# Score products of a causal attention, cut into two halves of 64 weight columns

## The chip, the cores and the metric

The kernel runs on one core of a Trainium2 chip. The metric is the device time of one execution in microseconds (us), taken as the median of several runs.

## The reference

The program is one block of a "macaron" transformer in f32: half a feed-forward step, attention, half a feed-forward step. The input x is 4 sequences of 1024 rows with 256 features.

```python
x = x + 0.5 * _L0_ffn_ref(_layernorm(x, axis=-1), ...)
x = x + _L0_attn_ref(_layernorm(x, axis=-1), ...)
x = x + 0.5 * _L0_ffn_ref(_layernorm(x, axis=-1), ...)

# in _L0_attn_ref: 16 heads of 16 features, rotary embedding on q and k
att = jnp.einsum('bhqd,bhkd->bhqk', q, k) / math.sqrt(hd)
mask = jnp.triu(jnp.full((T, T), -jnp.inf, dtype=att.dtype), k=1)
att = jax.nn.softmax(att + mask, axis=-1)
out = jnp.einsum('bhqk,bhkd->bhqd', att, v)
```

The feed-forward step is silu(x gate) * (x up), 704 wide, times a down matrix, with a scale for each output. What matters here is the product `q k` for each head, which contracts over only 16 features.

## The kernel before

**Tiling.** The 4096 rows are 8 blocks of 512 (`BLK`), two to a sequence. Heads lie in groups of four (`g`, 0 to 3): each head has 32 partitions (`HP`), of which 16 hold its features (`HD`). The tiles `qT` and `kT` hold queries and keys of a block in that form, features on partitions and rows on the free axis. In `qT`, a seventeenth row holds the negated maximum of each query's scores, and `kT` holds ones there.

**Scores are computed twice.** `max_half` computes scores with the query on the output partition, so that VectorE can take the maximum along the free axis: the weights are 128 columns of `qT`, the stream is up to 512 columns of `kT`. The maxima are turned by a small product (L939), copied, and sent into row 17 of `qT` by DMA. `exp_half` then computes the scores with the key on the output partition: the weights are 128 columns of `kT` with their row of ones, the stream is `qT`, and the maximum is subtracted by the product itself. ScalarE takes the exponential out of PSUM into `pT` (L981). `weigh` (L1019) multiplies `pT` with the values `va`, `attended` divides by the totals, and `project` applies Wo.

A unit of work covers four streams of 512 columns, one for each head of a group: a half has two heads (`pair` 0 or 1, `e` 0 or 1), and a burst places two halves of different pairs, so that the four heads' products stand on four different 32-row strips of TensorE. A half has one entry of 512 columns, or two entries (384 and 128, or 256 and 256) that share a PSUM bank. Each head's scores go to a bank of their own, `sc[e]`.

**The other products** go through `product_of`, which cuts the weights of 128 columns into four products of 32 columns (L470). These are the feed-forward products, the projections to q, k and v, and Wo. The products of `weigh` also have 32 weight columns, one head each. So TensorE works in two shapes for nearly the whole kernel: 32 rows by 128 columns for scores, 128 rows by 32 columns for the rest.

**Order.** The order of all instructions is fixed when the kernel is built. A planner (`Planner`) keeps an assumed clock for each engine, takes operations with an assumed duration `us`, and always places the one that can start first. For TensorE it adds assumed costs for a change between the shapes (`CHANGE`), and `burst` decides which two halves form the next visit to the scores: it waits for four free PSUM banks, and tends to place two bursts in a visit (`VISIT`). `plan.place` calls the operation's `emit`, which issues the instructions. The assumed duration of a half is `mm_us` of its columns. All of this is the same before and after the change.

The names that the change touches are `emit` in `max_half` (matmul at L859) and `emit` in `exp_half` (matmul at L972).

Of the kernel before, what the change touches and what calls it, by code (L numbers as in the profile page):

```python
# [19 lines left out]
P = 128  # L20
# [207 lines left out]
def mm_us(cols):  # L228
    return 4 * cols / 2400


def dve_us(n):
    return n / 960 + 0.07


def act_us(n, ptr=0):
    return n / 1200 + 0.09 + 0.09 * ptr
# [3 lines left out]
def tile_macaron(  # L241
# [16 lines left out]
    nc = tc.nc  # L258
# [9 lines left out]
    BLK = 512  # L268
    NB = BLK // P
# [7 lines left out]
        x=(6, [P, NB, D]),  # L277
        qT=(2, [P, NG, BLK]),
# [188 lines left out]
    def product_of(out, w, x, **kw):  # L467

        for m in range(w.shape[1] // HP):
            nc.tensor.matmul(out[ts(m, HP)], w[:, ts(m, HP)], x, **kw)  # L470

    def idle(d, n):

        for _ in range(n):
            nc.tensor.matmul(d.tile[:, :P], ident, ident, start=True, stop=True)
# [36 lines left out]
    def turned(pair, j, xnT, prio, later, view, idles=0):  # L512

        ds = [Buf("d") for _ in range(NC)]

        def emit():
            idle(ds[0], idles)
            for c, d in enumerate(ds):
                for n, (xn, _) in enumerate(pair):
                    nc.tensor.transpose(d.tile[:, ts(n, P)], xn.tile[:, ts(c, P)], ident)  # L520

        def copy(c):
            (nc.vector.tensor_copy if c else nc.scalar.copy)(
                view(xnT.tile[:, c])[:, j - 1 : j + 1],
                ds[c].tile[:, : 2 * P].rearrange("p (j a t) -> p j a t", j=2, t=HP),
            )

        t = Op("pe", 4 * 0.107, emit, [p[1] for p in pair], [*ds, xnT], [p[0] for p in pair], prio=prio, mode="full")
        k = [Op("act", act_us(D), partial(copy, 0), [t], uses=[ds[0], xnT], prio=later)]
        return t, [*k, Op("dve", dve_us(D), partial(copy, 1), [t], uses=[ds[1], xnT], prio=later)]  # L530
# [156 lines left out]
    qT = [Buf("qT") for _ in range(NBLK)]  # L687
# [156 lines left out]
    def row_at(g, part, h, j):  # L844

        return g % 2 * HP + part * GH * NB + h * NB + j

    def max_half(blk, unit, pair, nm, reduces):

        parts = 1 + blk % BPS  # L850
        sc = [Buf("score") for _ in range(2)]
        tiles = [kT[blk - parts + 1 + u[2]] for u in unit]

        def emit():

            for (g, j, _, c0, w, _), kt in reversed(list(zip(unit, tiles))):
                for e in range(2):
                    r = slice((2 * pair + e) * HP, (2 * pair + e) * HP + HD)
                    nc.tensor.matmul(  # L859
                        sc[e].tile[:, c0 : c0 + w],  # L860
                        qT[blk].tile[r, g, ts(j, P)],
                        kt.tile[r, g, :w],
                        start=True,
                        stop=True,
                    )

        gs = {u[0] // 2 for u in unit}
        need = [T_done[1, b, n] for b in range(blk - blk % BPS, blk + 1) for n in gs]
        first = Op(
            "pe", mm_us(sum(u[4] for u in unit)), emit, need, [*sc, nm], [qT[blk], *tiles], mode="row", tail=0.25  # L870
        )
        masked = [(c0 + w - P, c0 + w) for _, _, _, c0, w, m in unit if m]

        def head(e):
            prev = first
            if masked:

                def mask():
                    a, z = masked[0][0], masked[-1][1]
                    if masked[0][1] == masked[-1][0] or len(masked) == 1:  # L880
                        d = sc[e].tile[:, a:z].rearrange("p (m k) -> p m k", k=P)
                    else:
                        d = sc[e].tile.rearrange("p (m k) -> p m k", k=2 * P)[:, :, P:]
                    nc.vector.tensor_tensor(d, d, causal.unsqueeze(1).to_broadcast([P, len(masked), P]), ALU.add)  # L884

                prev = Op("dve", dve_us(P * len(masked)), mask, [first], uses=[sc[e]], prio=0, tail=0.1)
                loose_att.append(prev)

            if unit[0][0] != unit[-1][0]:
                j, part = unit[0][1:3]  # L890

                def reduce():
                    o = row_at(0, part, 2 * pair + e, j)
                    nc.vector.tensor_reduce(  # L894
                        nm.tile[:, o : o + HP + 1 : HP],
                        sc[e].tile.rearrange("p (g k) -> p g k", g=2),
                        AX.X,
                        ALU.max,
                        negate=True,
                    )  # L900

                o = Op("dve", dve_us(BLK), reduce, [prev, *filled["nm"]], uses=[sc[e], nm], prio=0, tail=0.25)
                loose_att.append(o)
                for g in (unit[0][0], unit[-1][0]):
                    reduces[g].append(o)
            else:
                for g, j, part, c0, w, _ in unit:

                    def reduce(g=g, j=j, part=part, c0=c0, w=w):
                        o = row_at(g, part, 2 * pair + e, j)  # L910
                        nc.vector.tensor_reduce(  # L911
                            nm.tile[:, o : o + 1], sc[e].tile[:, c0 : c0 + w], AX.X, ALU.max, negate=True
                        )

                    o = Op("dve", dve_us(w), reduce, [prev, *filled["nm"]], uses=[sc[e], nm], prio=0, tail=0.25)
                    loose_att.append(o)
                    reduces[g].append(o)

        for e in range(2):
            head(e)  # L920
        first.pair, first.kind = pair, "max"
        return first
# [38 lines left out]
    def exp_half(blk, unit, pair, pT, masks):  # L961
        base = blk - blk % BPS
        diag0 = blk % BPS * NB
        sc = [Buf("score") for _ in range(2)]
        tiles = [kT[base + k // NB] for _, k, _, _ in unit]
        w = sum(x[3] for x in unit)

        def emit():
            for (g, k, c0, w), kt in reversed(list(zip(unit, tiles))):
                for e in range(2):  # L970
                    r = slice((2 * pair + e) * HP, (2 * pair + e) * HP + HD + 1)
                    nc.tensor.matmul(  # L972
                        sc[e].tile[:, c0 : c0 + w],
                        kt.tile[r, g, ts(k % NB, P)],
                        qT[blk].tile[r, g, BLK - w :],
                        start=True,
                        stop=True,
                    )

        def weights(e):  # L980
            nc.scalar.activation(pT.tile[:, e, :w], sc[e].tile[:, :w], AF.Exp)  # L981

        need = [row_done[blk, g, pair] for g in sorted({u[0] for u in unit})]
        first = Op("pe", mm_us(w), emit, need, [*sc, pT], [qT[blk], *tiles], mode="row", tail=0.25)
        last = [Op("act", act_us(w), partial(weights, e), [first], uses=[sc[e], pT], prio=0, tail=0.25) for e in range(2)]
        loose_att.extend(last)
        done = list(last)
        for _, k, c0, _ in unit:
            if k >= diag0:

                def mask(c0=c0):
                    d = pT.tile[:, :, c0 : c0 + P]
                    nc.gpsimd.affine_select(  # L993
                        out=d,
                        in_=d,
                        compare_op=ALU.is_ge,
                        fill=0.0,
                        base=0,
                        pattern=[[0, 2], [1, P]],
                        channel_multiplier=-1,  # L1000
                    )

                last.append(Op("pool", 0.45, mask, done, uses=[pT], prio=0))
                loose_att.append(last[-1])
        masks.extend(last)
        first.pair, first.kind = pair, "exp"
        return first
# [297 lines left out]
```

## Time and profile before

| what | value |
|---|---|
| median of 3 runs | 1046.38 us (1046.28 to 1048.42) |
| profiled execution, its time | 1046.28 us |
| its span, first to last instruction | 1044.4 us |
| TensorE products: busy, instructions | 1036.3 us, 12162 |
| TensorE weight loads: busy, instructions | 442.7 us, 12162 |
| VectorE busy | 808.5 us |
| ScalarE busy | 429.7 us |
| GpSimd busy | 295.1 us |
| granted TensorE clock | 1.0 |

In the profile, PE stands for TensorE's products, PEld for its weight loads (issued by the same queue, able to overlap products), DVE for VectorE, ACT for ScalarE, POOL for GpSimd and SP for the queue that issues most DMAs. A group of instructions is written as line, engine, operation, output tile <- input tiles, then the shape: "17*128 17x512 f32" is a product with 17 rows and 128 columns of weights and 512 streamed columns. After the count come the busy time in us, the mean length of one in ns, and the time for which the engine was idle before them with what ended it. The length of a product counts from its own start to the modelled end of its last column, so products that follow each other closely overlap in the record.

### The profile page before, as it was taken

What the parts mean: (1) busy time and instruction counts of PE and PEld (TensorE: products, weight loads), DVE (VectorE), ACT (ScalarE), POOL (GpSimd) and SP (SyncE); (2) the same over time, 40 slices, a digit from 0 to 9 for tenths busy, and PEclk for the clock granted to TensorE, in tenths of its full rate; (3) what the DMA queues carried; (4) which work ended last, traced back from release to release, by engine and by line L of the source; (5) the groups of instructions that cost most, each with busy time, mean ns of one, the idle gap of its engine ahead of it and who ended that gap; (6) DMA issues with size and microseconds to landing.
All of it is one profiled execution on the core that took longest, in us unless ns stands there. A gap on an engine that the chain in (4) does not pass through costs nothing.

```text
span 1044.4 us, 28697 instructions
## 1 busy us (share of the span) xinstructions
PE 1036.3 (99%) x12162; PEld 442.7 (42%) x12162; DVE 808.5 (77%) x1876; ACT 429.7 (41%) x821; POOL 295.1 (28%) x501
## 2 busy tenths in 40 slices
PE   9999999999999999999999999999999999999998
PEld 5434443343444444443434443342434443434443
DVE  6679889788898887888897798778896797884432
ACT  3314341444453452435454434544354444455411
POOL 5222542231121633312115424221226211112200
PEclk9999999999999999999999999999999999999999
DMA  7211202102020021111010103101012010010000
GB/s 290 62 42 38 66 3 62 42 2 62 22 42 23 12 61 34 37 48 22 32 52 8 37 2 72 32 13 52 3 38 50 22 39 22 12 52 3 21 22 22
DMA packets 37969, 41.10 MB, mean 39 GB/s; under 512 B 3985, under 2 KB 27729, under 8 KB 37713
## 3 DMA queue, kind: packets, MB, share of 16 engines
q1 hardware_dynamic: 37184, 38.81, 14.1%
q8 instruction: 95, 1.56, 0.6%
q10 hardware_dynamic: 656, 0.47, 0.2%
q14 instruction: 34, 0.27, 0.1%
HBM read 19.60 MB, written 15.20 MB: 33 GB/s over the span
## 4 chain that ended last, share of the span: by engine, by line
PE 92%; DVE 6%; DMA 1%; issue 0%; ACT 0%; SPq 0%; DVEq 0%
PE bank L470 54%; PE bank L859 17%; PE bank L1019 12%; PE bank L972 10%; DVE nm L911 1%; DVE bank L884 1%; DVE xs L491 1%; DVE nm L894 1%; PE bank L939 0%; DVE hT L626 0%; DVE ta L623 0%; DMA xd<-xs 0%; PE bank L520 0%; DVE ta L603 0%; DVE hL L606 0%
## 5 line engine op out<-in xcount | busy, mean ns | idle before, releaser
L981 ACT ACTIVATE pT<-bank 128x512 f32<-128x512 f32 x576 | 298.5, 603 | 307.5 <-PE bank L972 306.7
L911 DVE TENSOR_REDUCE nm<-bank 128x1 f32<-128x512 f32 (+2 forms) x640 | 330.3, 573 | 20.0 <-PE bank L972 17.8
L470 PE MATMUL bank<-xnT,wgu_sb 128*32 128x512 f32 (+1 forms) x2832 | 321.5, 592 | 0.3
L859 PE MATMUL bank<-kT,qT 16*128 16x512 f32 (+3 forms) x1536 | 286.8, 511 | 2.2 <-DVE x L1104 0.9
L972 PE MATMUL bank<-qT,kT 17*128 17x512 f32 (+3 forms) x1536 | 286.7, 514 | 0.0
L470 PEld LDWEIGHTS bank<-xnT,wgu_sb 128*32 128x32 f32 x2832 | 92.0, 109 | 194.6 <-issue 122.1
L993 POOL TENSOR_SCALAR_AFFINE_SELECT pT<-pT 128x256 f32<-128x256 f32 x256 | 99.1, 407 | 263.9 <-ACT pT L981 263.0
L859 PEld LDWEIGHTS bank<-kT,qT 16*128 16x128 f32 x1536 | 111.3, 184 | 141.7 <-issue 35.3
L470 PE MATMUL bank<-wd_sb,hT 128*32 128x256 f32 x2560 | 152.4, 379 | 0.0
L1019 PE MATMUL bank<-pT,va 128*32 128x512 f32 (+3 forms) x1536 | 137.5, 487 | 0.4 <-DVE nm L911 0.2
L884 DVE TENSOR_TENSOR bank<-bank,causal 128x256 f32<-128x256 f32 (+1 forms) x320 | 103.9, 370 | 20.3 <-PE bank L972 15.1
L972 PEld LDWEIGHTS bank<-qT,kT 17*128 17x128 f32 x1536 | 109.4, 184 | 9.4 <-issue 2.6
L470 PEld LDWEIGHTS bank<-wd_sb,hT 128*32 128x32 f32 x2560 | 85.4, 110 | 55.1 <-issue 2.6
L620 ACT ACTIVATE ta<-bank,gus_sb 128x512 f32<-128x512 f32 x80 | 55.0, 687 | 113.2 <-PE bank L470 100.8
L623 DVE SCALAR_TENSOR_TENSOR ta<-ta,bank 128x512 f32<-128x512 f32 x80 | 54.6, 683 | 44.4 <-ACT ta L620 43.6
L1019 PEld LDWEIGHTS bank<-pT,va 128*32 128x32 f32 x1536 | 51.7, 109 | 83.5 <-issue 59.9
L1058 POOL TENSOR_TENSOR oq<-oq 128x512 f32<-128x512 f32 x32 | 40.7, 1273 | 154.8 <-DVE oq L1055 151.9
L1055 DVE STREAM_TRANSPOSE oq<-bank 128x512 f32<-128x512 f32 x64 | 45.5, 711 | 35.1 <-PE bank L1019 34.5
L626 DVE SCALAR_TENSOR_TENSOR hT<-bank,gus_sb,ta 128x512 f32<-128x512 f32 x80 | 59.5, 744 | 16.7 <-PE bank L470 15.5
L652 DVE TENSOR_TENSOR x<-bank,x 128x256 f32<-128x256 f32 x64 | 26.8, 418 | 49.7 <-PE bank L470 49.3
L731 POOL TENSOR_TENSOR qs<-qs,rope_sb 128x512 f32<-128x512 f32 x32 | 40.8, 1277 | 79.7 <-DVE qs L728 60.0
L470 PE MATMUL bank<-xnT,wqkv_sb 128*32 128x512 f32 x512 | 60.6, 595 | 0.1
(61 smaller groups left out, 649.0 us busy)
## 6 DMA issues: line engine op xcount, KB each, us to landing
xd<-xs SPq DMA_DIRECT2D x84, 128.0 KB
xnT<-xd SPq DMA_DIRECT2D x21, 512.0 KB
kT<-qT SPq DMA_DIRECT2D x64, 64.0 KB
x<-in_x SPq DMA_DIRECT2D x7, 512.0 KB
out<-x SPq DMA_DIRECT2D x14, 256.0 KB
qT<-nmT SPq DMA_DIRECT2D x128, 2.0 KB
wgu_sb<-in_wgu SPq DMA_DIRECT2D x2, 512.0 KB
rope_sb<-in_rope SPq DMA_DIRECT2D x1, 1024.0 KB
```

The lines of the kernel that those rows point to most:

```text
L470: nc.tensor.matmul(out[ts(m, HP)], w[:, ts(m, HP)], x, **kw)
L620: nc.scalar.activation(a.tile, d.tile, AF.Tanh, scale=gus_sb[:, 0, c : c + 1])
L623: nc.vector.scalar_tensor_tensor(a.tile, a.tile, 1.0, d.tile, ALU.add, ALU.mult)
L626: nc.vector.scalar_tensor_tensor(hT[c].tile, e.tile, gus_sb[:, 1, c : c + 1], a.tile, ALU.mult, ALU.mult)
L859: nc.tensor.matmul(sc[e].tile[:, c0 : c0 + w], qT[blk].tile[r, g, ts(j, P)], kt.tile[r, g, :w], start=True, stop=True,)
L884: nc.vector.tensor_tensor(d, d, causal.unsqueeze(1).to_broadcast([P, len(masked), P]), ALU.add)
L911: nc.vector.tensor_reduce(nm.tile[:, o : o + 1], sc[e].tile[:, c0 : c0 + w], AX.X, ALU.max, negate=True)
L972: nc.tensor.matmul(sc[e].tile[:, c0 : c0 + w], kt.tile[r, g, ts(k % NB, P)], qT[blk].tile[r, g, BLK - w :], start=True, stop=True,)
L981: nc.scalar.activation(pT.tile[:, e, :w], sc[e].tile[:, :w], AF.Exp)
L993: nc.gpsimd.affine_select(out=d, in_=d, compare_op=ALU.is_ge, fill=0.0, base=0, pattern=[[0, 2], [1, P]], channel_multiplier=-1,)
L1019: nc.tensor.matmul(av.tile[ts(r, HP), BLK - w :], va[base + k // NB].tile[:, k % NB, h * VS : h * VS + HP], pTs[u, r // 2].tile[:, r % 2, ...
L1055: nc.vector.transpose(o.tile, av.tile)
```

## The change

A helper `scores` is added beside `product_of`. It issues a score product as two products with 64 weight columns each, the first into output partitions 0 to 63, the second into 64 to 127. Rows, streamed columns and PSUM bank stay the same. A burst of four heads then stands on eight tiles of 32 rows and 64 columns. Both score products call it; the planner's assumed durations are not changed.

```diff
+    def scores(out, w, x):
+
+        for m in range(2):
+            nc.tensor.matmul(out[ts(m, P // 2)], w[:, ts(m, P // 2)], x, start=True, stop=True)
+
...
                 for e in range(2):
                     r = slice((2 * pair + e) * HP, (2 * pair + e) * HP + HD)
-                    nc.tensor.matmul(
-                        sc[e].tile[:, c0 : c0 + w],
-                        qT[blk].tile[r, g, ts(j, P)],
-                        kt.tile[r, g, :w],
-                        start=True,
-                        stop=True,
-                    )
+                    scores(sc[e].tile[:, c0 : c0 + w], qT[blk].tile[r, g, ts(j, P)], kt.tile[r, g, :w])
...
                     r = slice((2 * pair + e) * HP, (2 * pair + e) * HP + HD + 1)
-                    nc.tensor.matmul(
-                        sc[e].tile[:, c0 : c0 + w],
-                        kt.tile[r, g, ts(k % NB, P)],
-                        qT[blk].tile[r, g, BLK - w :],
-                        start=True,
-                        stop=True,
-                    )
+                    scores(sc[e].tile[:, c0 : c0 + w], kt.tile[r, g, ts(k % NB, P)], qT[blk].tile[r, g, BLK - w :])
```

## The prediction

> **What bounds the kernel now.** I read the engine totals first, then the chain, then the groups of TensorE with shapes kept apart, then a timeline of one stretch of score products. The page says that TensorE is the bound from end to end:
>
> ```profile
> PE 1036.3 (99%) x12162; PEld 442.7 (42%) x12162; DVE 808.5 (77%) x1876; ACT 429.7 (41%) x821; POOL 295.1 (28%) x501
> ...
> PE 92%; DVE 6%; DMA 1%; issue 0%; ACT 0%; SPq 0%; DVEq 0%
> PE bank L470 54%; PE bank L859 17%; PE bank L1019 12%; PE bank L972 10%; DVE nm L911 1%; DVE bank L884 1%; DVE xs L491 1%; DVE nm L894 1%; PE bank L939 0%; DVE hT L626 0%; DVE ta L623 0%; DMA xd<-xs 0%; PE bank L520 0%; DVE ta L603 0%; DVE hL L606 0%
> ```
>
> The first line is busy time, share and count by engine; the others are the chain that ended last. TensorE holds 92% of the chain, the two score lines (L859, L972) 27%. A nanosecond saved inside TensorE's queue is worth about 0.92 ns of span; one added costs about a full one. But a busy TensorE need not stream columns all the time, so I looked for exposed weight loads in the shapes of the score products (count, busy us, mean ns of one, idle before):
>
> ```profile
> L972 PE MATMUL bank<-qT,kT 17*128 17x512 f32 x768 | 195.4, 632 | 0.0
> L859 PE MATMUL bank<-kT,qT 16*128 16x512 f32 x768 | 190.8, 627 | 0.7 <-DVE oq L1055 0.5
> L1019 PE MATMUL bank<-pT,va 128*32 128x512 f32 x768 | 97.5, 595 | 0.4 <-DVE nm L911 0.2
> L859 PE MATMUL bank<-kT,qT 16*128 16x128 f32 x256 | 29.1, 311 | 0.4 <-DVE hT L626 0.4
> L972 PE MATMUL bank<-qT,kT 17*128 17x128 f32 x256 | 28.7, 315 | 0.0
> ```
>
> The score products of 512 columns last 30 to 40 ns longer on average than the products with 32-column weights at L1019, at the same streamed length. The timeline of one stretch (start us, length us) shows why:
>
> ```profile
> 505.71 0.70 PE L859 MATMUL bank<-kT,qT 16*128 16x512 f32 x2
> 505.72 0.70 PE L972 MATMUL bank<-qT,kT 17*128 17x512 f32 x2
> 506.24 0.59 PE L859 MATMUL bank<-kT,qT 16*128 16x512 f32 x2
> 506.26 1.01 PE L972 MATMUL bank<-qT,kT 17*128 17x512 f32 x4
> 506.69 0.59 PE L859 MATMUL bank<-kT,qT 16*128 16x512 f32 x2
> 507.11 0.59 PE L972 MATMUL bank<-qT,kT 17*128 17x512 f32 x2
> 507.12 0.59 PE L859 MATMUL bank<-kT,qT 16*128 16x512 f32 x2
> ```
>
> Each product stands there twice: the 192 one-entry halves of L972 issue 384 products of 512 columns and the group has 768 records. So an f32 product is two passes, each with a weight load of its own. Four passes, one on each 32-row tile, run together. The second four begin 0.53 us after the first, the later ones 0.43 us apart: 512 columns stream in 0.427 us, and the first four wait 0.106 us for their own weights, which nothing hides. Later loads lie beside the stream before them. In the same view narrowed to this stretch, the first four last 692 ns and the others 587.
>
> [...] 106 ns extra for 128 columns in the first pass of a score stretch, 26 ns for 32 columns in the first pass after a change back to the 32-column products (median of the starts in both cases; 617 against 592 ns in length). [...] no run so far shows tiles cut both ways, nor two passes each on them. [...] The trace shows some 94 ns from the end of the stream to the first score load, and 89 ns on the way back. [...]
>
> **The change, part by part.** The stretches of score products number 155, from the starts of all TensorE records in the trace. They hold 288 bursts of four streams with 512 columns each, 288 x 0.853 = 245.8 us of streaming in all.
>
> *Streaming* is meant to stay: twice the products, each on half the columns of the array, eight at a time instead of four. Cost 0 if eight tiles run together, covered by nothing if they don't.
>
> *Weight loads* halve from 128 to 64 columns. The exposed time comes from the group means. An unexposed pass is 588 ns for 512 columns (587 in the stretch shown), 374 for 256, 270 for 128, the medians or lower quartiles of their records. Four passes run together, so each sum is divided by 4:
> - 512 columns: 768 x (632 - 588) + 768 x (627 - 588) = 63.7 us, /4 = 15.9 us
> - 256 columns: 256 x (394 - 374) + 256 x (392 - 374) = 9.7 us, /4 = 2.4 us
> - 128 columns: 256 x (315 - 270) + 256 x (311 - 270) = 22.0 us, /4 = 5.5 us
> - 384 columns: 482 against 481, nothing.
>
> That is 23.9 us of exposed loads, [...] once for each of the 155 stretches and some 70 more inside, where a burst's banks came late. [...] **Saved: 12.0 us.** Bounds: all 12.0, or 0 if the two loads of one row group go one after the other.
>
> *Issue.* Products of a group start 6.7 ns apart (four within 20 ns in the records). Eight take 47 ns, so a stretch's last tile starts 27 ns later, and the change of mode has to wait for it: **155 x 27 = +4.1 us**. Inside a stretch each tile goes on at its own pace and nothing is added.
>
> *More instructions.* Score passes go from 3072 to 6144, and so do their loads: 6144 instructions more on 24,324. A burst of 512 columns needs 16 passes in 0.853 us, 53 ns per pass; the 256-column down products already run 54 ns per pass for microseconds. Bursts with two entries (96 of 288) need 27 ns, which the trace shows only over a few groups. [...] I take 0, with up to +3 us.
>
> *Change of mode.* 94 and 89 ns are drains and should stay. The trace has no 32x64 mode; I take 0 and give it 10 ns either way on 310 changes, 3 us.
>
> *Other engines.* The order on every engine stays as it is, since durations in the planner are untouched. VectorE and ScalarE see their first bank up to 50 ns sooner and do nothing new. No DMA is added but the fetch of instructions, 6144 x 64 bytes.
>
> Sum: -12.0 + 4.1 = -7.9 us on TensorE, times 0.92 = **-7.2 us**. The profiled execution took 1046.28 us (span 1044.4, 1.9 around it) against a median of 1046.38, so both stand for the same. Predicted: 1046.3 - 7.2 = **1039.1 us**; with the bounds above 1034 to 1043.
>
> **Rivals.**
> *Loads of a row group share their way in.* If the second column half of a row group loads after the first (53 + 53 ns), the exposed time stays and the issue cost comes on top: +4.1 us, 1050 us. Against it: the 32-column products load on four column tiles at once with only 26 ns exposed. Half way between, nothing measurable is left.
>
> *The two halves of a row group run in one queue.* This is the case on the slower side. Product one is low and high pass, then product two. If TensorE keeps order within a row group, half two's first pass starts only beside half one's second. Streams still overlap afterwards, so each stretch ends one pass later: 155 x 0.427 = +66 us, 1112 us. Its gain and loss balance at 7.9 / 0.427 = 18 stretches: from about an eighth of the 155 on, it decides. If halves didn't overlap at all, score streaming would double, +246 us. For it: no two-way tiles in this trace. Against: in both present modes the passes of other tiles overtake a waiting second pass (four first passes in 20 ns, with their second passes between them in program order).
>
> *The change does nothing*, with loads hidden anyway: 1046 us. The 692 against 587 ns speak against it.
>
> **How the numbers follow.** Two-way tiles run freely and loads halve: 0.66, 1039 us. Half gained, half lost to issue, or no effect: 0.11, about 1046. Shared loads: 0.11, 1050. One queue or worse: 0.12, 1112 and up. A measurement of this kernel tells about 0.2%, 2 us, from no change. Faster 0.66, same 0.11, slower 0.23. The range takes in the first three cases, from the bound of the first to just above the shared loads: 1033 to 1051; the likeliest case alone spans 1034 to 1043.
>
> **What would show it.** Right: score passes of 512 columns, first of a stretch, near 640 ns, later ones 588; the second group of eight about 0.48 us after the first; eight starts within some 47 ns; 64-column loads near 134 ns (an estimate between the 109 of 32 columns and the 184 of 128); 15,234 TensorE passes; the span of TensorE shorter by some 8 us with VectorE's busy time unchanged. Wrong: first passes of the second halves starting 0.43 us after the first halves', first passes still at 690 ns, or gaps at changes of mode away from 94 and 89 ns.

## The result: 0.6% slower, and the profile after

The changed kernel takes 1053.64 us (median, 1052.96 to 1054.4) against 1046.65 us for the kernel before: a ratio of 1.0063, 95% interval 1.005 to 1.0076. The profiled execution took 1052.96 us with a span of 1051.2, so 6.8 us more than the span before. The forecast was 1039.1 us with a range that ended at 1051: the wrong direction, and outside the range.

The page of the changed kernel, engine totals and the chain that ended last by engine and line:

```profile
PE 1043.2 (99%) x15234; PEld 424.0 (40%) x15234; DVE 809.6 (77%) x1876; ACT 430.4 (41%) x821; POOL 295.3 (28%) x501
...
PE 92%; DVE 5%; DMA 1%; ACT 1%; issue 1%; SPq 0%; DVEq 0%
PE bank L470 54%; PE bank L475 27%; PE bank L1012 11%; DVE nm L910 1%; DVE bank L883 1%; PE bank L938 1%; DVE xs L496 0%; DVE nm L893 0%; DVE oq L1048 0%; DVE ta L628 0%; DMA xd<-xs 0%; DVE hT L631 0%; PE bank L525 0%; DVE ta L608 0%; DVE hL L611 0%
```

Both score products now stand on line 475. Busy TensorE rose by 6.9 us (1036.3 to 1043.2), which is the whole loss; VectorE and ScalarE are as before. The weight loads grew from 12162 to 15234 and yet are busy for 19 us less. So the change did what it says to the loads, and something else on TensorE cost more.

The groups of TensorE with shapes kept apart, score products of 512 and of 128 columns (count, busy us, mean ns of one, idle before):

```profile
L475 PE MATMUL bank<-qT,kT 17*64 17x512 f32 x1536 | 194.7, 609 | 0.0
L475 PE MATMUL bank<-kT,qT 16*64 16x512 f32 x1536 | 186.8, 607 | 1.0 <-DVE oq L1048 0.7 <-DVE hT L631 0.2
L475 PE MATMUL bank<-qT,kT 17*64 17x128 f32 x512 | 31.0, 292 | 0.0
```

A mean of 609 and 607 ns stands where 632 and 627 stood. In the stretch whose timeline the prediction shows, the same view narrowed to its first group gives 638 ns for each of the eight passes, where the four had 692:

```profile
L475 PE MATMUL bank<-kT,qT 16*64 16x512 f32 x4 | 0.7, 638 | 0.0
L475 PE MATMUL bank<-qT,kT 17*64 17x512 f32 x4 | 0.7, 638 | 0.0
```

Each product is shorter, and still the engine needs longer. A mean length can't show this: the lost time is time in which some of the eight tiles run and others stand idle, and it appears in no idle column. So I laid the starts of all TensorE records of both traces side by side. Both have the same 320 visits to a shape in the same order, 155 of them score stretches. From before to after, the 32-column stretches changed by -0.5 us in all, the gaps between stretches by 0.0, **the score stretches by +7.45 us**. Sorted by the number of instructions (products and loads) that a stretch has after the change:

| instructions in the stretch | stretches | change in all, us | median, ns |
|---|---|---|---|
| 32 | 10 | -0.26 | -27 |
| 48 | 4 | 0.01 | -13 |
| 64 | 63 | -1.53 | -24 |
| 80 | 5 | +0.68 | +111 |
| 96 | 60 | +6.46 | +104 |
| 112 | 5 | +0.77 | +191 |
| 128 | 8 | +1.32 | +182 |

The sign turns between 64 and 80. Up to 64 instructions the change is the gain that was forecast in kind (-1.78 us over 77 stretches); above, it is a loss (+9.23 us over 78). The long stretches are those with bursts in which a half has two entries. One of them, with two bursts of 512 beside 256+256, in the timeline of before (start us, length us, number of records):

```profile
218.57 0.70 PE L859 MATMUL bank<-kT,qT 16*128 16x512 f32 x2
218.59 0.70 PE L972 MATMUL bank<-qT,kT 17*128 17x256 f32 x4
219.11 0.59 PE L859 MATMUL bank<-kT,qT 16*128 16x512 f32 x2
219.12 0.80 PE L972 MATMUL bank<-qT,kT 17*128 17x256 f32 x6
219.55 0.60 PE L859 MATMUL bank<-kT,qT 16*128 16x512 f32 x2
219.76 0.59 PE L972 MATMUL bank<-qT,kT 17*128 17x256 f32 x4
219.99 0.59 PE L859 MATMUL bank<-kT,qT 16*128 16x512 f32 x2
220.19 0.38 PE L972 MATMUL bank<-qT,kT 17*128 17x256 f32 x2
220.51 0.42 PE L470 MATMUL bank<-wd_sb,hL 128*32 128x256 f32 x4
```

and in that of the changed kernel:

```profile
219.00 0.66 PE L475 MATMUL bank<-kT,qT 16*64 16x512 f32 x4
219.02 0.66 PE L475 MATMUL bank<-qT,kT 17*64 17x256 f32 x8
219.48 0.61 PE L475 MATMUL bank<-kT,qT 16*64 16x512 f32 x4
219.50 0.78 PE L475 MATMUL bank<-qT,kT 17*64 17x256 f32 x9
219.94 0.61 PE L475 MATMUL bank<-kT,qT 16*64 16x512 f32 x4
220.10 0.64 PE L475 MATMUL bank<-qT,kT 17*64 17x256 f32 x6
220.37 0.60 PE L475 MATMUL bank<-kT,qT 16*64 16x512 f32 x4
220.41 0.82 PE L475 MATMUL bank<-qT,kT 17*64 17x256 f32 x9
221.16 0.42 PE L470 MATMUL bank<-wd_sb,hL 128*32 128x256 f32 x4
```

From the first score product to the first product of the next kind it took 1.94 us before and 2.16 after. The x9 in the fourth line is the key: of the second burst's first 256-column passes one starts in time, at 0.91 us after the stretch's start, and the other three only from 220.10 on, after 1.10 to 1.16 us. Meanwhile the 512-column heads of the second burst began in time, at 219.94. Nothing in the trace names a wait for these three.

Counting loads and passes in program order shows what they share. The first burst has 48, the 512-column half of the second 16. Numbered from 0, the late passes are instructions 69, 73 and 77; the one in time is 65. That led to a theory with a number in it.

### The profile page after: what moved, and what is told of

Its sections match the earlier page's. It is cut to its first block, busy times and chain, and to the rows that moved or that the text cites. A ratio compares the mean times of both kernels' runs of the same rounds, so it can differ in the third digit from the quotient of the medians.

```text
span 1051.2 us, 34891 instructions
## 1 busy us (share of the span) xinstructions
PE 1043.2 (99%) x15234; PEld 424.0 (40%) x15234; DVE 809.6 (77%) x1876; ACT 430.4 (41%) x821; POOL 295.3 (28%) x501
## 3 DMA queue, kind: packets, MB, share of 16 engines
q8 instruction: 119, 1.95, 0.8%
## 4 chain that ended last, share of the span: by engine, by line
PE 92%; DVE 5%; DMA 1%; ACT 1%; issue 1%; SPq 0%; DVEq 0%
PE bank L470 54%; PE bank L475 27%; PE bank L1012 11%; DVE nm L910 1%; DVE bank L883 1%; PE bank L938 1%; DVE xs L496 0%; DVE nm L893 0%; DVE oq L1048 0%; DVE ta L628 0%; DMA xd<-xs 0%; DVE hT L631 0%; PE bank L525 0%; DVE ta L608 0%; DVE hL L611 0%
## 5 line engine op out<-in xcount | busy, mean ns | idle before, releaser
L475 PE MATMUL bank<-qT,kT 17*64 17x512 f32 (+3 forms) x3072 | 291.1, 498 | 0.0
L475 PE MATMUL bank<-kT,qT 16*64 16x512 f32 (+3 forms) x3072 | 281.2, 495 | 1.9 <-DVE x L1097 0.8
L475 PEld LDWEIGHTS bank<-kT,qT 16*64 16x64 f32 x3072 | 84.4, 130 | 152.0 <-issue 37.8
L475 PEld LDWEIGHTS bank<-qT,kT 17*64 17x64 f32 x3072 | 93.5, 130 | 10.4 <-issue 2.5
```

The costliest lines, as they stand in the source:

```text
L475: nc.tensor.matmul(out[ts(m, P // 2)], w[:, ts(m, P // 2)], x, start=True, stop=True)
```

## The experiments

**Theory Q, queue:** TensorE holds 64 instructions and gives up a place only in program order. The first product of the stretch is 512 columns long. Its second pass, number 3, starts at 0.48 us and streams for 0.43 us; until it ends, at 0.909 us, the window can't move on, and the instructions that then enter start at 1.10 us, some 0.19 us later. The 64 is an estimate from the starts in this stretch: number 66, a load, starts at 0.913 us, too soon after that end to be one of those, and number 68, a load too, only at 1.100. Counted from number 3, that makes 64 or 65. **Rival R, rate:** instructions arrive too slowly for twice as many products. **Rival S, shape:** two entries of one half disturb each other on tiles cut both ways.

### The order woven, with 64 and with 128 columns (e1, e2)

```diff
+                rounds = max(h.parts for h in halves)
+                turns = [(k, h) for k in range(rounds) for h in sorted(halves, key=lambda h: -h.parts) if k < h.parts]
                 for h in halves:
                     h.us = us
+                    h.emit = lambda: None
+                halves[-1].emit = lambda: [h.part(k) for k, h in turns]
+                for h in halves:
                     self.place(h, at)
...
```

`part(k)` issues one entry of a half; both `emit` functions become such a `part` (not shown). Where one half has two entries and the other has one, the order is then: first entry, the other half, second entry. 

> Eight tiles as in the changed kernel, with one thing moved: in a burst where one half has two entries and the other has one, the program order is entry one, the other half, entry two, in place of one half after the other. Same instructions, same count. Theory Q (TensorE's queue holds 64 instructions, gives up a slot only in program order, and takes some 0.19 us to fill a slot again): the long stretches lose nothing any more, each of the 155 gains about 25 ns, the kernel takes about 1042.5 us (3 to 4 us under the kernel before). Theory R (instructions reach TensorE too slowly, whatever their order): it stays at 1053 to 1054 us. Theory S (two entries of one half get in each other's way on their tiles): it stays at 1053 to 1054 us too.

 

> The kernel before, four tiles and 128 columns, with the same woven order as the eight-tile kernel of this call. No stretch has over 64 instructions here. Theory Q, R and S: within 0.2% of before, 1045 to 1048 us; were it as fast as the woven eight-tile kernel, the order and not the 64 columns would be what gains.

Measured: woven with 64 columns 1043.71 us, ratio to before 0.9981 (0.9969 to 0.9993). Woven with 128 columns 1044.21 us, ratio 0.9978 (0.9971 to 0.9986). The page of the first, its engine totals:

```profile
PE 1031.7 (99%) x15234; PEld 417.6 (40%) x15234; DVE 808.6 (78%) x1876; ACT 430.2 (41%) x821; POOL 295.9 (28%) x501
```

The same 15234 products and as many loads keep TensorE busy 11.5 us less than in the changed kernel. The timeline of the stretch from above, woven:

```profile
217.50 0.45 PE L480 MATMUL bank<-qT,kT 17*64 17x256 f32 x4
217.53 0.66 PE L480 MATMUL bank<-kT,qT 16*64 16x512 f32 x4
217.76 0.61 PE L480 MATMUL bank<-qT,kT 17*64 17x256 f32 x8
...
218.41 0.61 PE L480 MATMUL bank<-kT,qT 16*64 16x512 f32 x4
218.43 0.61 PE L480 MATMUL bank<-qT,kT 17*64 17x256 f32 x8
...
219.41 0.42 PE L475 MATMUL bank<-wd_sb,hL 128*32 128x256 f32 x4
```

Both halves of the second burst start together, 0.91 us in, and the stretch lasts 1.92 us. Over the trace, the 78 long stretches went from +9.23 us against before to -3.14, the short ones from -1.78 to -1.99. The traced execution was the fastest of eight, 1042.01 us; by the medians the kernel is 2.5 us under the one before, not the 3 to 4 expected. Nothing but the order differs, so R and S can't have been the loss.

The second run is a miss: I had expected no change. The woven order is worth 2.0 us with 128 columns too. In the traces against each other, 64 columns are then worth 2.8 us of the score stretches, but the medians lie only 0.5 us apart and the intervals overlap, so end to end no difference is shown between the two.

### 64 columns in the short stretches alone, and in the long ones alone (e3, e4)

```diff
...
-        for m in range(2):
-            nc.tensor.matmul(out[ts(m, P // 2)], w[:, ts(m, P // 2)], x, start=True, stop=True)
+        n = 2 if plan.cut else 1
+        for m in range(n):
+            nc.tensor.matmul(out[ts(m, P // n)], w[:, ts(m, P // n)], x, start=True, stop=True)
```

`plan.cut` is set for each stretch from a list of the 155 (e3: up to 64 instructions, e4: over 64). 

> 64 columns on eight tiles only in the 77 stretches that have at most 64 instructions after the split; the other 78 keep 128 columns on four tiles. Q: the 77 gain 1.8 us in all and the others are as before: about 1044.6 us. R: the short stretches need their instructions just as fast, so that a gain would be due to a full queue at their start; also 1044 to 1046. S: the short stretches with two entries gain nothing.

 

> The reverse: eight tiles only in the 78 stretches that have over 64 instructions after the split. Q, R and S: +9.2 us in those, so about 1055.6 us, above the changed kernel. Below 1053 would mean that the loss does not belong to these stretches.

Measured: 1044.21 us, ratio 0.998 (0.9971 to 0.9989), and 1054.14 us, ratio 1.0075 (1.0062 to 1.0088). Together the two edits are the change, and they part it into a gain and a loss. In e4's trace the long stretches lost 8.6 us, the short ones changed by -0.1. Part of e3's 2.0 us is not the edit: it has -0.53 us in one long stretch that had waited for something else before. The loss belongs to the long stretches.

### TensorE alone: even and mixed bursts of different length (e5)

> Nothing of the block is computed: x is copied to the output, and TensorE runs score-like stretches without any wait on another engine, between runs of 32-column products of 512 columns. Each pattern four times, with four tiles of 128 columns and with eight of 64: even bursts (all heads with the same entries) of 512, 256+256 and 128 x4; mixed bursts (one pair of heads with 512, the other with 256+256 or 128+384), in turn and woven. Q: even bursts run at full rate at any length with eight tiles (853 ns per burst of four heads; 512 x3 and x4, 96 and 128 instructions, too); two mixed bursts in turn with eight tiles lose about 0.2 us against four tiles and woven ones lose nothing; one mixed burst loses nothing. R: even bursts of 256+256 and of 128 x4 fall behind with length, woven or not [...]. S: every burst with two entries loses, woven or not.

From the first score load to the end of the last stream, in ns, with the number of instructions on eight tiles in brackets; the four repetitions agreed within 2 ns but for the even bursts of 128:

| pattern | four tiles of 128 | eight tiles of 64 |
|---|---|---|
| even 512, 1 burst | 982 | 956 |
| even 512, 4 bursts (128 instructions) | 3557 | 3530 |
| even 256+256, 4 bursts (256 instructions) | 3577 | 3550 |
| even 128 x4, 4 bursts (512 instructions) | 3692 | 5524 to 6100 |
| 512 beside 256+256, 1 burst (48) | 986 | 960 |
| 512 beside 256+256, 2 bursts in turn (96) | 1850 | 2048 |
| the same woven | 1841 | 1814 |
| 512 beside 128+384, 2 bursts in turn (96) | 1860 | 2047 |
| the same woven | 1847 | 1856 |
| 512 beside 256+256, then even 512, in turn (80) | 1846 | 2043 |

Even bursts of 512 and of 256+256 gain 26 or 27 ns in all three rows. Past 64 instructions, at 128 and at 256, they lose nothing; all their tiles advance together, so the oldest products end as soon as any, and that is what Q asks for. It takes the order too: here the entries of the two halves alternate. In the changed kernel, where one half follows the other, the eight stretches that have two-entry halves alone lost 182 ns each (median). Two mixed bursts of 512 beside 256+256 lose 198 ns in turn and gain 27 woven. With no wait on another engine in this program, the loss lies in TensorE alone. S is out, since 256+256 beside itself takes 3550 ns for four bursts on eight tiles and 3577 on four. Woven bursts with 128+384 gain nothing, 1856 against 1847, which comes up again below.

The even bursts of 128 columns are a case of their own. On eight tiles they ran at 13.6 ns per pass for 159 to 255 passes and then stood once for 1.2 to 2.0 us. In all four repetitions a block of 16 KB of instructions was fetched around that time (the profile's DMA queue q8): the fetch began 0.9 to 1.3 us before the halt and took 1.0 to 1.4 us, and the halt ended 1.3 to 1.5 us after it. That fits R, instructions that come too late, but no run tests it. The granted clock fell to 0.5 during the halt or within 0.7 us after it, and at no other point between the first and the last product, so the length of these stretches holds more than the halt. In the score stretches of the changed kernel no gap between passes is longer than 0.5 us.

### The depth itself, and the half with two entries first (e6, e7, e8)

```diff
-                rounds = max(h.parts for h in halves)
-                turns = [(k, h) for k in range(rounds) for h in sorted(halves, key=lambda h: -h.parts) if k < h.parts]
+                turns = [(k, h) for h in sorted(halves, key=lambda h: -h.parts) for k in range(h.parts)]
```

This is the edit of e7 and e8, on the woven kernels; e6 is TensorE alone again. 

> Nothing of the block is computed: x is copied to the output, and TensorE runs short stretches on eight tiles without waits, between runs of 32-column products, each pattern four times. First patterns: two heads' products of 512 columns (16 instructions), then three rounds of 128 columns for the other two heads (48 instructions), then 0, 1, 2 or 4 more products of 128 columns, so 64, 68, 72 and 80 instructions. At full rate the extra products lie beside the 512 columns and all four take about 0.95 us. Q: 64 takes about 0.95 us; from 68 on the instructions past the queue's end come only when the first 512-column product has ended and reach TensorE some 0.19 us later, so about 1.3 us. R: a slow rise, some 50 ns for each product. S: no step. Last patterns: two mixed bursts (512 beside 256+256) in turn, with the two-entry half first, and woven. Q: 2.05 us in turn, about 2.0 with the two-entry half first (there the 512 columns of the second burst are the ones past the queue's end), 1.81 woven.

 

> Eight tiles of 64 columns; in a mixed burst the two-entry half comes first as a whole, then the other, not woven. Same instructions, same count. Q: the other half's second burst lies past the queue's end, long stretches still lose 0.1 to 0.2 us: 1050 to 1054 us. If starting the two-entry half first were all that the woven order does, 1043 to 1044 us.

 

> Four tiles of 128 columns with the two-entry half first, as a control for why the woven order gained 2 us with 128 columns as well. If it came from the start, since a half with two entries has one more load in a row and now starts up to 14 ns sooner: about 1044 to 1045 us. If it takes the other half between the two entries, as in the woven order: 1046 us. Q alone expects no change, since no stretch passes 64 instructions.

Measured for e6, first score load to last stream's end: 929 ns with 64 instructions, 1204 with 68, 1370 with 72, 1403 with 80; two mixed bursts 2047 in turn, 2049 with the two-entry half first, 1814 woven. The timeline of the stretches with 64 and with 68 instructions:

```profile
97.20 1.09 PE L55 MATMUL bank<-k,q 16*64 16x512 f32 x32
...
101.89 1.36 PE L55 MATMUL bank<-k,q 16*64 16x512 f32 x34
```

One product more, two passes of 128 columns, adds 0.27 us, although its tile had no other work from 0.74 us on. The record starts fit instruction by instruction. Numbered from 0, the extra product is 64 to 67: load, first pass, load, second pass. Its first load starts at 628 ns, its first pass at 735, its second load at 737; its second pass, number 67, starts at 1097. All this time the oldest instruction not done was number 3, the second pass of the first 512-column product, from 482 to 909 ns. 3 to 66 is a window of 64, and 1097 - 909 = 188 ns is what Q calls the time to fill a place again. The step is there, Q's number is right, and R's slow rise is not.

e7 took 1053.71 us, ratio 1.0066 (1.0052 to 1.008), as Q said: with the two-entry half first, the other half's second burst is what lies past 64. e8 took 1047.89 us, ratio 1.0013 (1.0006 to 1.0019), slower than before where Q expected no change, a second miss. So an early start is not what the woven order gains with 128 columns.

The traces say where e2's gain lies: in long stretches (-2.19 of -2.29 us). In ten of them the one-entry half's first load for the second burst starts 78 to 349 ns sooner than before, and the stretch is 78 to 122 ns shorter, 1.0 us in all. e8 is the reverse: in ten stretches that load starts at about 1002 ns in place of 667 to 778, and the stretch is 116 to 123 ns longer, 1.2 of the 1.7 us that its score stretches lost. Both steps are near the 106 ns of an exposed load of 128 columns, so the order may decide whether that load is hidden. But TensorE alone shows 9 to 13 ns for such a stretch with 128 columns, and no run tests it: what makes e2's gain stays open.

## Why the prediction was wrong

**What bounds the kernel, the drains, the other engines:** right. The loss is TensorE's own, the gaps at changes of shape are still 94 and 89 ns (medians; at none of the 310 changes, in either trace, did the next shape's first load come sooner than 93 and 86 ns after the last stream's end, with 427 ns for 512 columns), and VectorE's busy time moved by 1.1 us. The fetch of instructions (the page's queue q8) grew from 1.56 to 1.95 MB, the 6144 x 64 bytes of the forecast.

**Streaming on eight tiles:** right. Eight start within 47 ns (median), even bursts keep their rate (e5, four bursts of 512: 3530 ns against 3557), and the rival with one queue for both halves of a row group is out. So is the rival of shared loads: the first passes of a stretch have 50 ns exposed (638 against 588), not the 106 of two such loads in a row.

**Weight loads:** right in kind. A load took 130 ns (134 forecast), a first pass 638 (640 forecast), and the exposed time summed as in the prediction fell from 23.9 to 11.6 us. That half the columns save half the exposed time was an estimate; in the 65 stretches of 512 columns alone, the second group starts 533 ns after the first before the change and 480 after it (medians), 53 ns less. As a term of the span it was too large. The 70 exposures inside a stretch gave nothing: in the stretches of 512 columns alone the median gain is 27 ns with one exposed load (33 stretches) and 23 with more (32). In 29 of these 32 the second burst's first load came at the same time after the start of the stretch as before, within 3 ns (944 against 946 in one). The term is what each stretch has once, 53 ns, less the later start.

**Issue, +27 ns per stretch:** right. The first group's starts span 20 ns before and 47 after (medians). The net of both, 53 - 27 = 26 ns, is what e5 shows (27) and what the stretches of up to 64 instructions show (1.78 us / 77 = 23 ns). At best the change was then worth 155 x 0.026 = 4.0 us, not 7.9. The woven kernels reach less. Between their two traces 64 columns saved 2.8 us of the score stretches, of which 0.4 us is the net of two stretches that waited for something else (-0.73 and +0.33 us). Part of what is missing lies in the 40 stretches with two bursts of 512 beside 128+384, for which e5 has 9 ns more in place of 27 less: leaving out one that waited, they changed by -8 ns on average, and 13 of them grew by 14 to 30. The remainder is not accounted for.

**More instructions, "I take 0, with up to +3 us":** this is the step that failed. It asked only how fast instructions come, and found that fast enough. The question was which instructions TensorE holds at once. In e6 these are 64 (3 to 66), and number 67 started 188 ns after number 3 had ended. The kernel before has at most 64 instructions in any score stretch; the change doubles that, and 78 of 155 stretches pass it. The measured term is +9.23 us where these stretches would have gained about 78 x 0.026 = 2.0 us, so some 11 us against 0. A count of instructions per stretch, which the code gives, would have shown that no score stretch of before has more than 64, so that its trace says nothing of longer ones. The term also took 96 bursts to have two entries, as if two such halves always met. In the traces 124 bursts have one such half beside a half of 512 columns, as in the stretch shown above, and 34 have two.

None of the rivals was this one; the case at +66 us had the right place, TensorE's order, and the wrong mechanism.

## What to carry to other kernels

When an edit splits products on TensorE, count the instructions from one change of shape to the next in program order against the 64 of e6 (929 ns with 64, 1204 with 68). Then ask which old, long product holds the window while short ones on other tiles run dry. If tiles carry unequal lengths, issue their products in the order in which they will run, not one tile's whole list before the next: in e5 two bursts of 512 beside 256+256 took 1814 ns woven and 2048 in turn. And look for lost time in the starts of records: here the mean score product got shorter (632 to 609 ns) and the engine stayed 99% busy, while the score stretches took 7.45 us longer.

## What the runs showed of the hardware

- An f32 product's two passes stand together in program order, and first passes on other tiles start before its second one (all eight within 47 ns, the second pass at 482 in the stretch at 219.00 us), but in e6 only within 64 instructions of the oldest one that had not ended. The instruction past that started 188 ns after the end of the one that held the window (e6, 909 to 1097 ns), and a stretch of 68 instructions took 1204 ns against 929 with 64.
- After a change of shape, the second group of 512-column passes started 453, 480 and 533 ns after the first with 32, 64 and 128 f32 weight columns (medians in the two traces; the 64 stand on tiles cut both ways). Less the 427 ns of a stream in the forecast, an exposed load cost 26, 53 and 106 ns; less the 429 ns by which later score groups of the kernel before most often follow each other, 24, 51 and 104.
- Passes of 128 columns on eight tiles were issued every 13.6 ns for 159 to 255 passes and then halted once for 1.2 to 2.0 us (e5); the cause is not shown.
